# Two attention blocks on a batch of images: the order of score banks, the place of the layer statistics, and the place of the next image's norm

## The chip, the cores and the metric

The kernel runs on one core of one Trainium2 chip. The core has five engines with instruction streams of their own: TensorE (PE in the profile; its weight loads are PEld), VectorE (DVE), ScalarE (ACT), GpSimd (POOL) and SyncE (SP), which here only issues DMAs. They are tied together by semaphores. The metric is the device time of one execution in microseconds; a kernel's time is the median of several runs.

## What is computed

The input is a batch of 8 images, each 512 channels by 32 x 32 = 1024 positions, in 32-bit floats. Two attention blocks follow each other. Cut to what matters:

```
# layer 0: group norm over 32 groups, 8 heads of 64 channels
h   = group_norm(x, 32 groups)
qkv = w_qkv @ h + b_qkv                    # per image, 1x1 convolution
w   = softmax(q^T k / sqrt(64))            # per head, 1024 x 1024
x   = x + w_proj @ (w applied to v) + b_proj

# layer 1: group norm over 8 groups, one head of 512 channels
xn  = group_norm(x, 8 groups)
q, k, v = q_w @ xn + q_b, k_w @ xn + k_b, v_w @ xn + v_b
w   = softmax(q^T k / sqrt(512))
x   = x + p_w @ (w applied to v) + p_b
```

## The kernel before

**Matrix products by seven factors.** Nearly every product other than layer 0's attention is done by the scheme of Strassen and Winograd: a product of 2 x 2 blocks takes seven block products instead of eight, numbered 1 to 7, of sums and differences of blocks. `left_sums` and `right_sums` give those sums as lists of steps. `conv2` and `scores1` use the scheme twice, so that 7 outer products have 7 inner products each; `inner_steps` does the inner seven of one or two outer products, in the order 1, 6, 2, 5, 7, and leaves inner products 3 and 4 in the list `tail`. The next stage runs the tail behind its own first product (`finish`), so that TensorE has work while the first product's bank is copied. Inner products 1 and 2 use PSUM bank a, 6, 7 and 4 use b, 5 and 3 use c.

**PSUM.** Six of the eight banks are in three pools named a, b and c, two banks each, and two are in a pool `ps_acc` for small accumulations. `psum_pools` closes the three pools and opens them anew at the start of each stage, after it has run the tail. In the matrix products a tile is one bank, so each pool holds two tiles. In the attention a score tile takes the two banks of one pool, so that there are three score tiles in flight.

**Stages.** For image b, the main loop runs layer 0's attention (`attention0`), then the projection with the residual sum (`projection`), then, for image b-1, layer 1's first product g (`layer1_scores`), its scores (`scores1`), its values (`values1`), and then layer 0's values (`values`), keys and queries (`keys_and_queries`) for image b+1. For image 1 keys and queries are made in the turn of image 0, and then the function gets four hooks for the norm of layer 1. In all later turns it gets none.

**Layer 0's attention.** There are eight blocks, one for each pair of heads and half of the positions. A block makes eight score tiles (four matmul records each), takes the exponential of each on ScalarE, adds them up on VectorE, multiplies them with the values (32 matmul records), and sums over partitions (8 records). A counter n picks the pool of each score tile.

**Layer 1's statistics.** The group norm of layer 1 needs a mean and a variance of the projected image. `projection` gives them as a list `stats` of twelve steps for VectorE: eight half_stats (bn_stats over 512 positions, held in program order) and four end_stats (bn_aggr). By place in the list, 5, 7, 9 and 11 are end_stats. `scores1` deals the list out among its seven outer products. Its calls are `product(s, p, ...)`: s counts the calls, p is the number of the factor, and the fifth argument lists further factors that GpSimd makes. The argument `small` goes to the list `background`, of which one step is run behind each inner product. So a list that is given to one outer product is run from that product's inner product 6 on, one step at a time.

**Layer 0's norm of the image after next.** `values` puts the load and the statistics of image b+2 (tiles named ahead) into the background list. `keys_and_queries` then does the rest: `group_mean` is a small matmul on TensorE (gmean) and four VectorE steps on 128 x 4 numbers, `affine` is a second small matmul (gvar), one VectorE step and four GpSimd steps (the power -1/2 of the variance, the scale, the mean times scale, the shift). The scale and shift are used when that image is loaded for good and its norm is applied by ScalarE, in the turn after. A hook is a list of calls that `inner_steps` runs behind the inner product 7 of one of the four pairs of outer products of `conv2`; in the listing they are the argument `after7`.

**Order.** Instructions marked by `keep_in_program_order` keep the order in which the program writes them on their engine; all matmuls are among them. The others are placed by the builder's own scheduler.

Of the kernel before, what the change touches and what calls it, by code (L numbers as in the profile page):

```python
# [9 lines left out]
F32 = mybir.dt.float32  # L10
# [5 lines left out]
P = 128  # L16
# [13 lines left out]
def two_attention_blocks_kernel(  # L30
# [10 lines left out]
    KC = C // P  # L41
    HT = T // 2
# [29 lines left out]
    def pcols(name):  # L72
        i = 4 * PARAMS.index(name)
        return par[:, i : i + 4]
# [101 lines left out]
    def main_path(ctx):  # L176
# [14 lines left out]
        def acc_tile(name):  # L191
            return ps_acc.tile([P, HT], F32, tag="acc", name=name)


        ps_pools = []
# [408 lines left out]
        def attention0(b, q, k, v, a, extra):  # L604
            n = 0

            for hp in range(KC):
                for tb in (0, 1) if hp < KC - 1 else (1, 0):
                    uid = f"0_{b}_{hp}_{tb}"
                    total = pair_tile(f"sum_{uid}")  # L610
                    es = []
                    for s in range(NS):
                        sc = ps_pools[n % 3].tile([P, 2, HT], F32, tag="sc", name=f"sc_{uid}_{s}")
                        n += 1
                        for j in range(2):
                            matmul(
                                sc[:, j, :], k[hp][ts(j, 64), ts(s, P)], q[hp][ts(j, 64), ts(tb, HT)],
                                start=True, stop=True,
                            )
                        e = pair_tile(f"e_{uid}_{s}")  # L620
                        nc.scalar.activation(e, sc, AF.Exp, scale=(C // 8) ** -0.5)  # L621
                        if s == 1:
                            nc.vector.tensor_add(total, es[0], e)  # L623
                        elif s > 1:
                            nc.vector.tensor_add(total, total, e)  # L625
                        es.append(e)
                    for f in extra.pop(0) if extra else ():
                        f()
                    av = acc_tile(f"av_{uid}")
                    for s in range(NS):  # L630
                        for j in range(2):
                            matmul(
                                av[ts(j, 64), :], v[s // 2][:, s % 2, hp * P + j * 64 : hp * P + (j + 1) * 64],
                                es[s][:, j, :], start=(s == 0), stop=(s == NS - 1),
                            )
                    for f in extra.pop(0) if extra else ():
                        f()
                    dst = a[hp][:, ts(tb, HT)]
                    nc.scalar.copy(dst, av)  # L639

                    last = (hp, tb) == (KC - 1, 0)
                    r = reciprocals(total, uid, False, nc.scalar if last else nc.sync)
                    if not last:
                        nc.gpsimd.tensor_tensor(dst, dst, r, ALU.mult)  # L644
                    else:
                        scaled = lambda dst=dst, r=r: tc.keep_in_program_order(nc.vector.tensor_mul(dst, dst, r))

            assert not extra
            return scaled


        def scores1(f, gf, gsteps, first, uid, stats):

            scale = C**-0.5
            e = {(c, cc, r): pair_tile(f"e_{uid}_{c}{cc}{r}") for r in range(2) for c in range(2) for cc in range(2)}
            total = pair_tile(f"sum_{uid}")  # L660
            parts = [pair_tile(f"sum{r}_{uid}") for r in range(2)]
            g2 = {1: first}

            def factors(p):
                g2[p] = query_factors(gf[p], f"{p}_{uid}")

            def blocks(at, r, cc):
                return [e[at[1], cc, at[0]][:, :, ts(r, 2 * P)]]

            def add(dst, ps, x):  # L670
                nc.vector.tensor_add(dst[0], ps, x[0])  # L671

            def more(dst, x, y, r, cc):

                tc.keep_in_program_order(
                    nc.gpsimd.tensor_tensor(blocks(dst, r, cc)[0], blocks(x, r, cc)[0], blocks(y, r, cc)[0], ALU.add)
                )

            def exps(r, c):
                for cc in (1, 0):  # L680
                    nc.scalar.activation(e[c, cc, r], e[c, cc, r], AF.Exp, scale=scale)  # L681

            def add_up(r, c):

                on = lambda dst, x, y: lambda: tc.keep_in_program_order(nc.gpsimd.tensor_tensor(dst, x, y, ALU.add))  # L685
                if r == c:
                    return [on(parts[r], e[c, 0, r], e[c, 1, r])]
                return [
                    *(on(parts[r], parts[r], e[c, cc, r]) for cc in range(2)),
                    on(total[:, r, :], parts[r][:, 0, :], parts[r][:, 1, :]),  # L690
                ]

            def product(s, p, y, x, before, small, after7=(), final=()):
                def mm(ps, j, start):
                    for i in range(2):
                        matmul(
                            ps[:, i, :], f[p][j][:, ts(i, P)], g2[p][j], start=start and i == 0, stop=True, skip_group_check=True
                        )

                def extra(r, cc, read, written):  # L700

                    if p == 6 and written:
                        more((0, 1), (1, 0), (1, 1), r, cc)
                    if p == 7 and written:
                        more((1, 1), (1, 0), (1, 1), r, cc)

                inner_steps(
                    f"{uid}_{s}", s % 2, 2, mm, add, lambda *at: blocks(y, *at), x and (lambda *at: blocks(x, *at)),
                    extra, after7, final, [lambda: background.extend(small), *(lambda q=q: factors(q) for q in before)],
                )  # L710

            product(0, 1, (1, 0), None, [2], stats[:3] + gsteps[:2])
            product(1, 2, (0, 0), (1, 0), [5], gsteps[2:4], (), [lambda: exps(0, 0)])
            product(2, 5, (1, 1), None, [6, 4], gsteps[4:] + stats[3:6])
            product(3, 6, (1, 0), (1, 0), [7, 3], stats[6:7])
            product(4, 7, (1, 0), (1, 0), [], stats[7:9])
            product(5, 3, (0, 1), (0, 1), [], stats[9:11] + add_up(0, 0), [lambda: exps(1, 1)], [lambda: exps(0, 1)])
            product(
                6, 4, (1, 0), (1, 0), [], stats[11:] + add_up(1, 1) + add_up(0, 1), (),
                [lambda: exps(1, 0), lambda: background.extend(add_up(1, 0) + steps)],  # L720
            )

            t = [[pair_tile(f"t{n}_{uid}_{cc}") for cc in range(2)] for n in (1, 2, 4)]
            engines = [nc.vector] * 4 + [nc.gpsimd] * 4
            fs, steps = right_sums(
                [(e[0, cc, 0], e[0, cc, 1]) for cc in range(2)], [(e[1, cc, 0], e[1, cc, 1]) for cc in range(2)],
                [lambda cc, n=n: t[n][cc] for n in range(3)],
                lambda *a: engines.pop(0).tensor_tensor(*a, ALU.subtract),
            )
            return total, {p: [x[:, i, :] for x in fs[p] for i in range(2)] for p in fs}  # L730
# [142 lines left out]
        v, q, k, norm0, later = prologue()  # L873
# [78 lines left out]

        def keys_and_queries(b, f, norm, hooks):

            k = conv2("k", f, None, f"k0_{b}", hooks)
            hooks = [[all_background], [], []]
            if norm:
                hooks[1].append(lambda: norm.group_mean(acc_tile(f"gmean_0_{b + 1}")[:, :KC]))
                hooks[2].append(lambda: norm.affine(acc_tile(f"gvar_0_{b + 1}")[:, :KC]))
            q = conv2("q", f, pcols("bq0"), f"q0_{b}", hooks)  # L960
            return q, k

        def layer1_scores(b, inner):
# [31 lines left out]
        for b in range(B):  # L995
# [33 lines left out]
            if b > 0:  # L1029
# [4 lines left out]
                norm1, stats = projection(b, af, xt, [scaled, steps[7]])  # L1034
                gf, gsteps = layer1_scores(b - 1, inner)
                _, _, mean, affine = norm_hooks(norm1, f"1_{b}")
# [6 lines left out]
                if b + 1 < B:  # L1043
                    hf, steps = image_factors(h, f"h0_{b + 1}")
                    background.extend(steps)
                    v, f, norm0 = values(b + 1, hf)
                    q, k = keys_and_queries(b + 1, f, norm0, ())
            elif B > 1:
                v, f, norm0 = values(1, hf, [[], [], [], [], [*steps[:7], scaled, steps[7]]])
                norm1, stats = projection(0, af, xt)  # L1050
                hooks = norm_hooks(norm1, "1_0")
# [216 lines left out]
```

## Time and profile before

| What | us |
|---|---|
| median of 3 runs | 2849.69 |
| lowest and highest run | 2848.17, 2850.7 |
| the profiled execution, device time | 2849.52 |
| its span, first to last instruction | 2847.7 |
| VectorE, sum of exponentials (L623, L625) | 600.9 busy |
| ScalarE, exponentials of layer 0 (L621) | 476.8 busy |
| TensorE, layer 0's score matmuls | 458.7 busy |
| TensorE, layer 0's value matmuls | 453.6 busy |

The granted TensorE clock is 0.999 over the span. In a group of the profile, names such as `psb_q<-inner_h,w_q` give the tile written and the tiles read: `psb_q` is bank b of the queries' convolution, `sc` a score tile, `e` its exponential, `sum` the running sum, `bnst` and `mv` the statistics. Timelines give the start in us from the span's beginning, the length, the engine, the line, the operation, the tiles, the shapes and the number of instructions merged into the line; in brackets stands how long the engine was idle before it and what ended that. In rows of windows the first pair is the stretch, then its length, and then the busy time and number of instructions of each engine, the granted clock, and the share and GB/s of the DMA engines. All matmuls have line L67, as they go through one helper. One matmul of 32-bit floats has two records.

### The profile page before, as it was taken

The numbers are of one execution on the slowest core, as the hardware profiler recorded it, in microseconds if no ns is written. First come the engines' busy times: TensorE is split into PE (matmuls) and PEld (weight loads), VectorE is DVE, ScalarE is ACT, GpSimd is POOL, SyncE is SP. The second block draws the span as 40 slices with busy tenths as digits, with TensorE's granted clock in tenths as the row PEclk, the third lists the DMA queues.
The fourth block names the chain that finished last, engine by engine and source line by source line (L and its number), as shares of the span: only waits on it lengthen the run. The fifth ranks groups of instructions, "written<-read, shape, count | busy, mean of one in ns | idle before, by whom it ended". The sixth has DMA issues, their size and how long they took to land.

```text
span 2847.7 us, 32456 instructions
## 1 busy us (share of the span) xinstructions
PE 2827.0 (99%) x11846; PEld 1690.0 (59%) x11846; DVE 2083.8 (73%) x2733; ACT 929.0 (33%) x1177; POOL 1205.4 (42%) x1193
## 2 busy tenths in 40 slices
PE   9999999999999999999999999999999999999998
PEld 5435635866367653677537674376743868338584
DVE  5587787766877678776787757877578775887765
ACT  1252452214522145220552215422154311633130
POOL 2123215732167321673227722277123761147672
PEclk9999999999999999999999999999999999999999
DMA  8632403133031230322213232122311223012301
GB/s 276 190 127 90 180 20 126 36 144 134 20 144 65 106 128 26 134 94 97 109 49 111 94 118 92 49 108 97 134 72 49 107 101 142 35 52 94 121 2 68
DMA packets 91597, 280.59 MB, mean 99 GB/s; under 512 B 10595, under 2 KB 36387, under 8 KB 82470
## 3 DMA queue, kind: packets, MB, share of 16 engines
q1 hardware_dynamic: 89638, 276.15, 26.7%
q10 hardware_dynamic: 1792, 2.29, 0.2%
q8 instruction: 96, 1.57, 0.2%
q14 instruction: 71, 0.58, 0.1%
HBM read 227.31 MB, written 51.09 MB: 98 GB/s over the span
## 4 chain that ended last, share of the span: by engine, by line
PE 97%; DVE 2%; issue 1%; ACT 0%; POOL 0%; DVEq 0%; POOLq 0%; ACTq 0%
PE sc L67 16%; PE av L67 16%; PE psb_av L67 6%; PE psb L67 5%; PE psa_av L67 4%; PE psc_av L67 4%; PE psc L67 3%; PE psa L67 3%; PE psb_z L67 3%; PE psb_p L67 3%; PE psb_v L67 3%; PE psb_k L67 3%; PE psb_g L67 3%; PE psb_q L67 2%; PE psa_p L67 2%; PE psa_z L67 2%
## 5 line engine op out<-in xcount | busy, mean ns | idle before, releaser
L625 DVE TENSOR_TENSOR sum<-sum,e 128x1024 f32<-128x1024 f32 x384 | 522.4, 1360 | 41.8 <-DVE sum L623 1.4
L621 ACT ACTIVATE e<-sc 128x1024 f32<-128x1024 f32 x512 | 476.8, 1053 | 73.2 <-PE sc L67 72.3
L67 PE MATMUL sc<-q,k 64*128 64x512 f32 x2048 | 458.7, 596 | 0.5
L67 PE MATMUL av<-e,v 128*64 128x512 f32 x2048 | 453.6, 596 | 0.0
L67 PEld LDWEIGHTS sc<-q,k 64*128 64x128 f32 x2048 | 193.3, 186 | 239.2 <-ACT e L621 104.0
L67 PEld LDWEIGHTS av<-e,v 128*64 128x64 f32 x2048 | 141.4, 137 | 304.3 <-issue 304.3
L588 POOL TENSOR_TENSOR all_recs<-all_recs,rc 128x256 f32<-128x256 f32 x72 | 65.2, 905 | 528.3 <-DVE rc L586 520.7
L644 POOL TENSOR_TENSOR a<-a,r 128x512 f32<-128x512 f32 x56 | 112.6, 2010 | 265.0 <-DMA r<-rows 220.8
L586 DVE RECIPROCAL rc<-sums 128x256 f32<-128x256 f32 x72 | 126.4, 1756 | 46.4 <-PE sums L67 26.5
L532 POOL TENSOR_TENSOR k<-k,k 128x256 f32<-128x256 f32 x28 | 20.0, 727 | 315.8 <-DVE u_k L527 315.8
L639 ACT COPY a<-av 128x512 f32<-128x512 f32 x64 | 37.4, 585 | 318.2 <-PE av L67 318.2
L623 DVE TENSOR_TENSOR sum<-e,e 128x1024 f32<-128x1024 f32 x64 | 78.5, 1226 | 58.9 <-ACT e L621 58.9
L67 PE MATMUL psb<-inner,inner_h 128*128 128x256 f32 x448 | 116.1, 382 | 1.2 <-DVE u L671 0.5
L67 PE MATMUL psa_av<-e,z 128*128 128x512 f32 x256 | 113.3, 596 | 0.0
L140 ACT ACTIVATE h<-h,b,s 128x1024 f32<-128x1024 f32 x62 | 78.4, 1268 | 93.9 <-DMA h<-in_x 77.3
L411 POOL TENSOR_TENSOR inner_h<-h,inner_h 128x256 f32<-128x256 f32 x120 | 106.8, 892 | 2.2
L67 PEld LDWEIGHTS psb<-inner,inner_h 128*128 128x128 f32 x448 | 83.9, 190 | 16.9 <-POOL inner L426 3.8
L411 POOL TENSOR_TENSOR inner_h<-h 128x256 f32<-128x256 f32 x60 | 58.8, 979 | 78.5 <-ACT h L140 78.5
L685 POOL TENSOR_TENSOR sum<-sum,e 128x1024 f32<-128x1024 f32 x32 | 76.2, 2380 | 27.5 <-ACT e L681 26.2
L67 PE MATMUL psb_g<-inner_h,w_m 128*128 128x256 f32 x336 | 86.0, 383 | 0.3
L411 POOL TENSOR_TENSOR inner_h<-t_h 128x256 f32<-128x256 f32 x90 | 77.9, 868 | 10.8 <-PE psc_av L67 9.5
L67 PEld LDWEIGHTS psa_av<-e,z 128*128 128x128 f32 x256 | 48.0, 190 | 57.2 <-issue 56.6
(344 smaller groups left out, 5535.4 us busy)
## 6 DMA issues: line engine op xcount, KB each, us to landing
x<-in_x SPq DMA_DIRECT2D x36, 512.0 KB
h<-in_x SPq DMA_DIRECT2D x32, 512.0 KB
spill<-x SPq DMA_DIRECT2D x32, 512.0 KB
h<-spill SPq DMA_DIRECT2D x32, 512.0 KB
x<-spill SPq DMA_DIRECT2D x32, 512.0 KB
out<-x SPq DMA_DIRECT2D x64, 256.0 KB
w_p<-sums_p SPq DMA_DIRECT2D x8, 1792.0 KB
r<-rows SPq DMA_DIRECT2D x112, 128.0 KB
```

What stands on the lines that cost most here:

```text
L67: tc.keep_in_program_order(nc.tensor.matmul(*args, **kw))
L140: tc.keep_in_program_order(nc.scalar.activation(dst, src, AF.Identity, bias=b, scale=s))
L411: pin(nc.gpsimd.tensor_tensor(dst, x, y, ALU.subtract))
L532: nc.gpsimd.tensor_tensor(d, x, y, ALU.add)
L586: nc.vector.reciprocal(rc, sums)
L588: nc.gpsimd.tensor_tensor(all_recs, all_recs, rc, ALU.add)
L621: nc.scalar.activation(e, sc, AF.Exp, scale=(C // 8) ** -0.5)
L623: nc.vector.tensor_add(total, es[0], e)
L625: nc.vector.tensor_add(total, total, e)
L639: nc.scalar.copy(dst, av)
L644: nc.gpsimd.tensor_tensor(dst, dst, r, ALU.mult)
L685: on = lambda dst, x, y: lambda: tc.keep_in_program_order(nc.gpsimd.tensor_tensor(dst, x, y, ALU.add))
```

## The change

Three edits, all in how the same work is ordered.

1. In `attention0`, the score tile's pool is chosen by (0, 2, 1)[n % 3] instead of n % 3.
2. In `scores1`, the twelve steps of `stats` are dealt out otherwise. The call with factor 6 gets none where it had one. The call with factor 5 gets two instead of three, that with factor 7 two, that with factor 3 three instead of two, that with factor 4 two instead of one.
3. In `keys_and_queries`, where no hooks are given, the next image's `group_mean` moves from the hook behind the second pair of the queries to that behind the first pair of the keys, together with the call that empties the background list; `affine` moves from the third pair of the queries to the fourth pair of the keys. Where hooks are given (image 1), all stays.

```
-                        sc = ps_pools[n % 3].tile([P, 2, HT], F32, tag="sc", name=f"sc_{uid}_{s}")
+
+                        sc = ps_pools[(0, 2, 1)[n % 3]].tile([P, 2, HT], F32, tag="sc", name=f"sc_{uid}_{s}")
...
-            product(2, 5, (1, 1), None, [6, 4], gsteps[4:] + stats[3:6])
-            product(3, 6, (1, 0), (1, 0), [7, 3], stats[6:7])
-            product(4, 7, (1, 0), (1, 0), [], stats[7:9])
-            product(5, 3, (0, 1), (0, 1), [], stats[9:11] + add_up(0, 0), [lambda: exps(1, 1)], [lambda: exps(0, 1)])
+            product(2, 5, (1, 1), None, [6, 4], gsteps[4:] + stats[3:5])
+            product(3, 6, (1, 0), (1, 0), [7, 3], [])
+            product(4, 7, (1, 0), (1, 0), [], stats[5:7])
+            product(5, 3, (0, 1), (0, 1), [], stats[7:10] + add_up(0, 0), [lambda: exps(1, 1)], [lambda: exps(0, 1)])
             product(
-                6, 4, (1, 0), (1, 0), [], stats[11:] + add_up(1, 1) + add_up(0, 1), (),
+                6, 4, (1, 0), (1, 0), [], stats[10:] + add_up(1, 1) + add_up(0, 1), (),
...
-            k = conv2("k", f, None, f"k0_{b}", hooks)
-            hooks = [[all_background], [], []]
+            mean, affine = [], []
             if norm:
-                hooks[1].append(lambda: norm.group_mean(acc_tile(f"gmean_0_{b + 1}")[:, :KC]))
-                hooks[2].append(lambda: norm.affine(acc_tile(f"gvar_0_{b + 1}")[:, :KC]))
-            q = conv2("q", f, pcols("bq0"), f"q0_{b}", hooks)
+                mean.append(lambda: norm.group_mean(acc_tile(f"gmean_0_{b + 1}")[:, :KC]))
+                affine.append(lambda: norm.affine(acc_tile(f"gvar_0_{b + 1}")[:, :KC]))
+            if hooks:
+                k = conv2("k", f, None, f"k0_{b}", hooks)
+                q = conv2("q", f, pcols("bq0"), f"q0_{b}", [[all_background], mean, affine])
+            else:
+
+                k = conv2("k", f, None, f"k0_{b}", [[all_background, *mean], [], [], affine])
+                q = conv2("q", f, pcols("bq0"), f"q0_{b}")
             return q, k
```

## The prediction

> **What bounds the kernel now.** I read the page first, for the engine that carries the span, and then the chain of waits.
>
> ```profile
> span 2847.7 us, 32456 instructions
> PE 2827.0 (99%) x11846; PEld 1690.0 (59%) x11846; DVE 2083.8 (73%) x2733; ACT 929.0 (33%) x1177; POOL 1205.4 (42%) x1193
> PE 97%; DVE 2%; issue 1%; ACT 0%; POOL 0%; DVEq 0%; POOLq 0%; ACTq 0%
> ```
>
> TensorE is the bound from end to end: 2827.0 of 2847.7 us busy and 97% of the chain. No edit of the change takes a matmul away. So it can win only where a matmul starts late. The ends of matmuls are modelled, so late starts show in the distance between starts, not as idle time. I therefore asked for the timeline of TensorE at each place that the change touches, first the start of an attention (image 3):
>
> ```profile
> 1028.38 7.48 PE L67 MATMUL sc<-q,k 64*128 64x512 f32 x32
> 1035.79 7.09 PE L67 MATMUL av<-e,v 128*64 128x512 f32 x32
> 1042.80 0.64 PE L67 MATMUL sums<-sum,ones 128*32 128x256 f32 x8
> 1043.37 7.14 PE L67 MATMUL sc<-q,k 64*128 64x512 f32 x32
> ```
>
> A block is 32 score matmuls, 32 value matmuls and 8 for the sums. The first block's scores take 7.48 us, the next one's 7.14 us. From first score to first score, the first block takes 1043.37 - 1028.38 = 14.99 us, and the second (1058.03 in the same view) 14.66 us. Narrow timelines there show who is late:
>
> ```profile
> 1028.38 1.13 PE L67 MATMUL sc<-q,k 64*128 64x512 f32 x4
> 1028.56 0.87 DVE L525 SCALAR_TENSOR_TENSOR q<-psb_q,par,q 128x256 f32<-128x256 f32 x2
> 1029.58 0.70 PE L67 MATMUL sc<-q,k 64*128 64x512 f32 x2
> ```
>
> The first score tile, four matmuls, starts at 1028.38. The second starts at 1029.58, 1.20 us later, where one tile in the steady run takes 0.86 us (7.14 us over eight tiles, less the last matmul's modelled tail). VectorE empties bank b of the queries until 1028.56 + 0.87 = 1029.43, and the second score tile lies in b. Its start follows that end by 0.15 us.
>
> [...]so a score tile has to wait for the reader of its own bank and for no other. The trace agrees: the wait is for b, while c was empty at 1028.45. [...]the trace shows none waiting (idle before gmean and gvar 0). [...]the norm's d x d product has a median of 1.08 us, and 0.16 us where GpSimd was idle.
>
> **Part 1, the order of banks.** The rotation a, b, c becomes a, c, b; no instruction is added or removed. The queries' convolution ends with product 3 in c and then product 4 in b, so b is the last to come free. The new second tile lies in c, which VectorE leaves at 1027.57 + 0.88 = 1028.45; its turn is 1029.24 or a little later, so it does not wait. The new third tile lies in b, free for TensorE at 1029.58, and its turn is 1030.1 or later: half a microsecond of room. The gain is one late start for each attention that follows a queries' convolution through b, the seven images 1 to 7. First block against second, from the starts, they are 14.99 or 15.00 against 14.65 or 14.66 us: 0.34 us each, 7 x 0.34 = 2.4 us. The attention of image 0 follows other matmuls, and its first block already takes 14.66 us: no gain there.
>
> What is late next? ScalarE's exponentials follow each other at 0.90 us and the score tiles at 0.86, so a tile of the first block could find its bank not read yet. The steady blocks run with the same three banks and the same 0.90 us at 14.66 us a block, so the first block can become a steady one and no better. VectorE's sum of the block must end before the sums matmuls. It begins when the second exponential ends, 0.1 us earlier too, and its seven passes fit in the steady block. At the attention's end 32 value matmuls (7.1 us) lie between the last score tiles and the next user of the banks. Nothing there.
>
> **Part 2, statistics out of the product with factor 6.** One bn_stats (0.68 us on VectorE) leaves product 6, and each later one moves a product on; the last lands in the product with factor 4. The count stays twelve. Windows over layer 1's scores (window, width, TensorE busy) give the price: an image with statistics, then the last image, which has none:
>
> ```profile
> 2237.20:2277.80 40.60, 40.45 (x186) 1.00 0.12 46
> 2723.02:2763.63 40.61, 40.15 (x185) 1.00 0.00 1
> ```
>
> With or without statistics 40.6 us: VectorE has the room. No matmul of product 6 starts late. Of eight images, two take 40.73 us, from a late start in the tail of product 7, 0.13 us each; the statistic there is replaced by another one in the same slot, so I let it stay. The new last statistic stands ahead of at most two VectorE sums in the product with factor 4, whose next TensorE reader is a longer product away (eight matmuls of 0.216 us). The layer's mean comes after it with room: in image 2 the last aggregate is at 878.33 us, one product (6.0 us) later is 884.4, and the mean's matmul is at 892.73. So 0, between -0.6 (the two images' 0.13 each, and 0.34 that one image takes longer still) and +0.7 us (0.1 for each of seven images).
>
> **Part 3, the norm in the keys' convolution.** It concerns the images whose norm comes in this function without other hooks: 2 to 6, five of them. Moved are two pairs of tiny matmuls on TensorE, five small VectorE operations (0.15 to 0.20 us each), four small GpSimd ones (about 1.7 us together) and no DMA; the call that empties the background list moves too. Windows over the queries' convolution of image 6, with the norm, and of image 7, without it, then over the keys' of image 6:
>
> ```profile
> 2048.99:2073.07 24.08, 24.03 (x112) 20.09 (x110) 15.16 (x40) 7.23 (x12) 7.18 (x13) 1.00 0.64 240
> 2396.92:2420.61 23.69, 23.64 (x107) 19.63 (x106) 14.66 (x35) 7.24 (x12) 5.71 (x9) 1.00 0.64 244
> ...
> 2022.26:2048.99 26.73, 26.73 (x123) 22.96 (x122) 15.54 (x34) 4.41 (x8) 5.58 (x8) 1.00 0.33 121
> ```
>
> The norm costs the queries 24.08 - 23.69 = 0.39 us. The starts say what that is: twice 0.14 us for a pair of tiny matmuls and 0.08 us of slower start behind it, less 0.05 us where a later wait is shorter. In the keys the same two pairs cost the same. Net 0, if VectorE has room and the statistics are ready.
>
> Both are in the trace of image 3:
>
> ```profile
> 978.24 0.20 DVE L103 BATCH_NORM_AGGREGATE mv<-bnst 128x2 f32<-128x12 f32 x1
> ...
> 989.11 0.69 DVE L527 TENSOR_TENSOR k<-psb_k,c_k 128x512 f32<-128x512 f32 x1 [2.83 <-PE psb_k L67]
> 990.84 0.69 DVE L527 TENSOR_TENSOR k<-psc_k,u_k 128x512 f32<-128x512 f32 x1 [1.03 <-PE psc_k L67]
> ...
> 998.48 1.42 POOL L532 TENSOR_TENSOR k<-k,k 128x256 f32<-128x256 f32 x2 [46.33 <-DVE u_k L527]
> ```
>
> The mean's matmul would stand at 988.84, behind product 7 of the first pair; its statistics are done at 978.44, ten microseconds before. VectorE is idle 1.03 us between its two sums there, and GpSimd for 46 us, so the mean's four VectorE steps (0.74 us by their starts at 1017.20 in the queries) run unhindered and end before or just as the next sum is due. A bank emptied 0.2 us late is wanted two products later. The second half stands at the keys' last pair, where VectorE again waits 0.97 us for TensorE and GpSimd has nothing left, so the scale and shift are made sooner than now. Their reader, the next image's apply, is a whole attention away. The background list has run empty during the values' convolution (19 entries, four a step), so emptying it early adds nothing. I take 0, between -1.1 us (the stall of about 0.22 us behind the queries' third pair, five times, if the norm caused it; against that, image 7 has it too) and +1.0 us (a sum 0.2 us late, five times).
>
> **The sum.** -2.4 + 0 + 0 = -2.4 us against the profiled execution's 2849.52 us (span 2847.7 and 1.8 around it): 2847.1. That execution lies 0.17 us below the median of the runs, 2849.69, so against the median it is 2847.3, which I take: 0.08% faster. Differences within 0.2% (5.7 us) I count as the same, about what a measurement of this kernel can tell from no change.
>
> **The rivals.**
> - All parts pay. The bank's 2.4, part 2's 0.6 and part 3's 1.1 us: 2845.6. For it: VectorE is the late one in the queries' last pairs, and the norm works there. Against: image 7's starts show the same late ones without the norm. Chance 0.17.
> - The bank's gain is handed back: the score tiles then wait for exponentials, or the sums for VectorE, 2849.7. For it: 0.90 against 0.86 us. Against: the steady blocks. Chance 0.12.
> - Slower: the mean's matmul finds its statistics not ready in the keys' convolution[...]. Place: the end of the first pair of the keys. It decides from the point where the last aggregate comes after the tenth microsecond past 978.44. The load that feeds it already made VectorE wait 5.2 us in this image; a landing 12 us later would cost 2 us in each of five images: -2.4 + 10 = +7.6, 2857.3. Against: the aggregate ends within a microsecond of the keys' start in all five images. Chance 0.04.
> - Instructions that aren't held in program order find other places, since the kernel's builder orders them by its own estimate, and VectorE meets GpSimd at other times. One 7.8 us VectorE product at 943.76 us, beside a run of GpSimd subtractions, cost TensorE about 1 us in one image alone. I price it at one such event per layer-1 image, 7 us, either way: 2840.3 or 2854.3. Chance 0.12, more of it below, as the late starts that could go are many and small (0.66 us an image in the scores).
>
> **How the numbers follow.** The forecast itself has 0.55. Its own range is the three bounds added: 2847.3 - 1.7 and + 1.7, so 2845.6 to 2849.0. The range for the time takes in "all parts pay" and "handed back", with a little of the spread of the runs (2848.17 to 2850.7): 2844.6 to 2849.9. Faster by over 0.2% (below 2844.0) needs the last rival's good side, and some of the first with a low run: 0.11. Slower by over 0.2% (above 2855.4): 0.04 for the late statistics and 0.01 for the last rival's other side: 0.05. Within: 0.84.
>
> **What would show it.** Part 1 right: the first block's 32 scores read 7.14 us in all eight images, and VectorE's last sum from b ends before the third tile's turn. Handed back: a first block of 14.99 us with ScalarE or VectorE in front of the late matmul. Part 2: layer 1's scores stay at 40.6 us. Part 3: the queries at 23.69 and the keys at 27.1 us; wrong if a gmean matmul in the keys shows idle time before it. The forecast falls if the kernels differ by more than 5 us, or elsewhere than in these three places.

## The result and the profile after

The changed kernel takes 2843.98 us (median of 20 runs, 2842.68 to 2845.52), the kernel before in the same session 2849.10 us (20 runs, 2848.02 to 2851.02). The ratio is 0.9982 with a 95% interval of 0.9976 to 0.9988: 5.1 us, or 0.18%, less. The forecast had the sign, and a difference within 0.2%. But its 2847.3 us promised 2.4 us, and the result lies 0.6 us below the low end of its range, 2844.6 us. About half of the gain was not in its sum. Another 0.6 us of the distance is the base: the forecast started from a median of 2849.69 us over three runs, and twenty runs give 2849.10 us.

The page of the changed kernel, the same three lines as shown of before (span; busy time by engine; shares of the chain of waits):

```profile
span 2841.1 us, 32477 instructions
PE 2824.5 (99%) x11846; PEld 1689.7 (59%) x11846; DVE 2082.5 (73%) x2733; ACT 928.1 (33%) x1177; POOL 1201.3 (42%) x1193
PE 97%; DVE 2%; issue 1%; POOL 0%; ACT 0%; DVEq 0%; POOLq 0%; ACTq 0%
```

TensorE is still the bound, with the same 11846 matmul records, and its busy time fell by only 2.5 us while the span fell by 6.6. So part of the gain is time in which TensorE did nothing. The profiled execution took 2842.86 us, 1.1 below the median, so the 6.6 us contain some luck. One more number of the page is worth a stop: 32477 instructions against 32456, in a change that adds none in the program's text. By the records all the difference is in semaphore instructions (EVENT_SEMAPHORE): 7 more on TensorE, 17 more on ScalarE, 6 more on GpSimd, 2 fewer on VectorE and 7 fewer on SyncE.

**The place of part 1.** TensorE's timeline at the attention of image 3, in the columns start, length, engine, line, operation:

```profile
1026.17 7.14 PE L67 MATMUL sc<-q,k 64*128 64x512 f32 x32
1033.23 7.09 PE L67 MATMUL av<-e,v 128*64 128x512 f32 x32
1040.25 0.64 PE L67 MATMUL sums<-sum,ones 128*32 128x256 f32 x8
1040.82 7.14 PE L67 MATMUL sc<-q,k 64*128 64x512 f32 x32
```

The first block's scores read 7.14 us instead of 7.48, and from first score to first score the block takes 1040.82 - 1026.17 = 14.65 us, like every other. A narrow timeline around its first three score tiles (twelve records) shows why. Before:

```profile
1028.38 3.19 PE L67 MATMUL sc<-q,k 64*128 64x512 f32 x12
```

and after:

```profile
1026.17 2.85 PE L67 MATMUL sc<-q,k 64*128 64x512 f32 x12
1026.34 0.88 DVE L525 SCALAR_TENSOR_TENSOR q<-psb_q,par,q 128x256 f32<-128x256 f32 x2
```

VectorE leaves bank b at 1026.34 + 0.88 = 1027.22. The tile in b is now the third, whose turn is at least two tiles of 0.86 us after 1026.17, so at 1027.89 or later. It does not wait. Nor does the second tile, in c: in the records its first matmul starts at 1027.13, 0.09 us before VectorE leaves b. The 3.19 - 2.85 = 0.34 us are the late start. The attentions of images 1 to 7 each became 0.338 to 0.344 us shorter, 2.39 us in all; that of image 0 kept its length.

**The place of part 3.** Windows over the keys and then the queries of image 6 (stretch, its length, busy time and count on PE, PEld, DVE, ACT and POOL):

```profile
2018.69:2045.79 27.10, 27.10 (x128) 23.35 (x126) 16.25 (x38) 4.41 (x8) 5.64 (x8) 1.00 0.33 119
2045.79:2069.50 23.71, 23.66 (x110) 19.74 (x108) 14.48 (x36) 7.24 (x12) 7.26 (x12) 1.00 0.64 243
```

They read 27.10 and 23.71 us where before had 26.73 and 24.08: the norm's 0.37 us has moved from one to the other. Both were forecast, 27.1 and 23.69. And the mean's matmul finds its statistics ready, in the timeline of image 3 (two lines of TensorE):

```profile
986.63 0.28 PE L67 MATMUL gmean<-mv,gm 128*128 128x4 f32 x2
986.77 0.68 PE L67 MATMUL psa_k<-h,w_k 128*128 128x256 f32 x2
```

and the mean's steps on VectorE with the next sum behind them:

```profile
987.51 0.15 DVE L115 COPY gmean<-gmean 128x4 f32<-128x4 f32 x1
987.70 0.16 DVE L117 TENSOR_TENSOR d<-mv,gmean 128x4 f32<-128x4 f32 x1
987.89 0.16 DVE L119 TENSOR_TENSOR d<-d 128x4 f32<-128x4 f32 x1
988.09 0.16 DVE L121 TENSOR_TENSOR dv<-d,mv 128x4 f32<-128x4 f32 x1
988.85 0.69 DVE L527 TENSOR_TENSOR k<-psc_k,u_k 128x512 f32<-128x512 f32 x1 [0.60 <-PE psc_k L67]
```

No idle time stands before gmean, and the four small steps (987.51 to 988.25) fit into a hole before VectorE's next sum: VectorE still waits 0.60 us for TensorE there.

**Where the rest lies.** The starts of the stages, one after another, before against after, give the whole shift of the profile:

| Place | shift, us |
|---|---|
| first weights, before any image's work | -0.91 |
| first blocks, seven attentions | -2.39 |
| norm: keys +0.37, queries -0.37, five images | 0.00 |
| the end of image 2's layer 1 and its values | -0.62 |
| layer 1's scores, two images, 0.13 each | -0.26 |
| small ones (image 5, image 7) | -0.27 |
| from the last matmul to the end | -2.22 |
| sum | -6.67 |

The first row is spread and no gain: a second profile of the kernel before is 0.37 us shorter there, and the statistics alone, which will turn out to gain nothing, 0.91 us. Two rows are large and were not in the sum: the end of image 2 and the end of the program. The experiments are about these.

### The profile page after: what moved, and what is told of

It is laid out like the page before. It is cut to its first block, busy times and chain, and to the rows that moved or that the text cites. A ratio compares the mean times of both kernels' runs of the same rounds, so it can differ in the third digit from the quotient of the medians.

```text
span 2841.1 us, 32477 instructions
## 1 busy us (share of the span) xinstructions
PE 2824.5 (99%) x11846; PEld 1689.7 (59%) x11846; DVE 2082.5 (73%) x2733; ACT 928.1 (33%) x1177; POOL 1201.3 (42%) x1193
## 3 DMA queue, kind: packets, MB, share of 16 engines
q1 hardware_dynamic: 89638, 276.15, 27.1%
q8 instruction: 96, 1.57, 0.2%
## 4 chain that ended last, share of the span: by engine, by line
PE 97%; DVE 2%; issue 1%; POOL 0%; ACT 0%; DVEq 0%; POOLq 0%; ACTq 0%
PE sc L67 16%; PE av L67 16%; PE psb_av L67 6%; PE psb L67 5%; PE psa_av L67 4%; PE psc_av L67 4%; PE psc L67 3%; PE psa L67 3%; PE psb_z L67 3%; PE psb_p L67 3%; PE psb_v L67 3%; PE psb_k L67 3%; PE psb_g L67 3%; PE psb_q L67 2%; PE psa_p L67 2%; PE psa_z L67 2%
## 6 DMA issues: line engine op xcount, KB each, us to landing
out<-x SPq DMA_DIRECT2D x64, 256.0 KB
```

## The experiments

### Each part alone, and the kernel before once more

The first three kernels have one of the three edits shown above each; the fourth is the unchanged kernel. First theory: the bank order alone brings the attentions' 2.4 us. The rivals credit the two other parts, or the timing of the engines against each other.

```
A  sc = ps_pools[(0, 2, 1)[n % 3]].tile(...)
B  the five product(...) calls with stats[...] dealt out anew
C  keys_and_queries with mean and affine in the keys' hooks
```

> The kernel before with the new order of banks alone. Theory 1 (each part as forecast, the missing 2.5 us lies outside the three parts or in one chance collision of VectorE and GpSimd): 2.4 us faster, ratio 0.9992; first blocks of the attentions of images 1 to 7 at 14.66 us. Theory 2 (the order of banks brings all of the 5.1 us, since the shifted phase also removes the 7.8 us VectorE product of image 2): 3.4 to 5 us faster, and that long product is gone in this profile. Theory 3 (the gain comes from the norm or the statistics): under 2.4 us.

> The kernel before with the new dealing of the layer-1 statistics alone. Theory 1: 0.3 us faster (two images of eight lose a late start of 0.13 us), ratio 0.9999, not to be told from no change; scores at 40.60 us in all images. Theory 3: 1 us or more faster. The 7.8 us VectorE product of image 2 stays under theory 1, unless it is a matter of chance from run to run.

> The kernel before with the norm moved to the keys alone. Theory 1: no change, ratio 1.0000; keys 26.73 + 0.45 us, queries 24.08 - 0.45 us. Theory 3: 1.5 to 2.5 us faster, either there or because the 7.8 us VectorE product of image 2 is gone.

> The kernel before, unchanged, against itself. Ratio 1.0000 within 0.0003 gives what a comparison of this kernel can tell. Its profile shows what in the first one is chance: under theory 1 the start (first matmuls of the weights, 0.98 us between the two profiles) and the end (6.96 us after VectorE's last operation against 4.74 us) differ from run to run; if they stay at the values of the first profile of the kernel before, they belong to the program.

The ratios are to the kernel before, run beside them.

| Kernel | median, us | ratio to before (2848.75 us) | span, us |
|---|---|---|---|
| bank order alone | 2844.57 | 0.9986 (0.9979 to 0.9992) | 2843.3 |
| statistics alone | 2848.16 | 0.9997 (0.9989 to 1.0006) | 2846.6 |
| norm alone | 2848.27 | 0.9998 (0.9990 to 1.0007) | 2847.0 |
| unchanged | 2849.0 | 1.0000 (0.9991 to 1.0008) | 2847.7 |

Parts 2 and 3 alone cannot be told from nothing. The bank order alone gives 4.2 us, nearly the whole gain. That is the size that theory 2 expected but not its cause, since the long VectorE product of image 2 is still there (7.81 us at 942.88). Its stage starts hold only the forecast 2.4 us in the seven attentions and 0.2 us elsewhere, up to the last matmul. The remaining 1.8 us of its profile come after that matmul. So the question was no longer which part, but what happens at the end. The timeline's last matmul and last VectorE instruction, before:

```profile
2838.46 0.19 PE L67 MATMUL ps_good<-ones,both 128*1 128x1 f32 x2
2840.02 0.75 DVE L748 SCALAR_TENSOR_TENSOR x<-o,obias,x 128x512 f32<-128x512 f32 x1
```

and with the bank order alone (the timeline's head gives the span, which is 2847.7 us before):

```profile
core 0 of [0], span 2843.3 us
...
2835.84 0.19 PE L67 MATMUL ps_good<-ones,both 128*1 128x1 f32 x2
2837.40 0.75 DVE L748 SCALAR_TENSOR_TENSOR x<-o,obias,x 128x512 f32<-128x512 f32 x1
```

VectorE's last sum ends 2.31 us after the last matmul's start in both (2840.02 + 0.75 - 2838.46; 2837.40 + 0.75 - 2835.84). But from there to the end of the span it is 2847.7 - 2840.77 = 6.9 us before, and 2843.3 - 2838.15 = 5.2 us with the new order. No calculation lies there; what runs is the end of TensorE's own program. Its instructions that do no arithmetic are in the trace, though not in the timelines. In us from the start of TensorE's last matmul record, which lies 0.03 us behind the start in the timeline, as records of the trace:

```
before        TENSOR_LOAD 0.86  COMPARE_BRANCH 1.46 (3.61 long)  EVENT_SEMAPHORE 5.12  DRAIN 8.49  EVENT_SEMAPHORE 8.67 ... end 9.25
bank order    TENSOR_LOAD 0.86  COMPARE_BRANCH 1.45 (3.75 long)  EVENT_SEMAPHORE 5.26  DRAIN 5.41  EVENT_SEMAPHORE 6.84 ... end 7.42
```

Before, 3.4 us pass between a semaphore instruction of 0.05 us and the next instruction; with the new order 0.15 us. The second profile of the unchanged kernel has the long end too (9.74 us), so it is not chance from run to run. And the counts of TensorE's records differ: 24085 before, 24092 with the bank order. The difference is seven EVENT_SEMAPHORE instructions (388 and 395), one in each attention of images 1 to 7. Where the second score tile alone waited for its bank in an instruction of its own (at 1029.47 in image 3), now the second and the third do (1027.72 and 1028.70 with the bank order alone). The statistics alone and the norm alone leave 24085.

This suggested that the end depends on where TensorE's last instructions lie in the packets of the queue for instructions. The page has "q8 instruction: 96, 1.57", packets and MB; by the records each packet has 16384 bytes. The first 94 of them go out one behind another while TensorE runs: in the kernel before, the first when 196 of its instructions have started and the 94th when 24005 have, so one packet in every 256.0 instructions on average (139 to 366 from one to the next); in the changed kernel 194 and 23979, one in every 255.8. From this comes an estimate: one packet stands for a block of 256 of TensorE's instructions. 24085 instructions at 256 a block are a little over 94 blocks, beside 96 packets.

The records of this queue hold the packets' times too. In us from the last matmul record again, the last two packets and what TensorE did next:

```
before        packet 2.47 to 3.66, branch ends 5.07;  packet 5.82 to 7.29, DRAIN 8.49
bank order    packet 2.46 to 3.74, branch ends 5.20;  DRAIN 5.41, packet 5.94 to 6.91
```

The first of these packets goes out during the branch in all thirteen profiles of this document, and the branch ends 1.4 to 1.5 us after it has landed. The second packet goes out in all of them too. Before, the DRAIN follows its landing by 1.2 us; with the bank order the DRAIN has run before this packet goes out. So the gap of the kernel before ends as the branch does, shortly after a packet has landed.

### Shifting the instructions without touching the work

If only the place in the block counts, a few instructions put ahead of the kernel before must shorten its end, with the banks in the old order. Two small matmuls whose result nothing reads were added before the first stage, 8 records in all. The three pairs of parts were run beside it.

```
+        for i in range(2):
+            matmul(acc_tile(f"pad{i}")[:, 0:1], ones, ones[:, 0:1], start=True, stop=True)
```

> The kernel before with two tiny matmuls added ahead of the first weights, while TensorE waits for its first load; nothing reads their result. They only make TensorE's program a few instructions longer, as the new order of banks does (seven semaphore instructions more on TensorE). Theory 1 (the 2.2 us at the end is a place in the program[...]): the end after the last matmul falls from 9.3 to 9.8 us to 7.0 to 7.5 us, and the kernel gets 2 us faster, ratio 0.9993, without any of the three edits. Theory 2 (the shorter end comes from the order of banks itself, or is chance): end and time as before, ratio 1.0000.

> Bank order and statistics, norm as before. Theory 1: 2.4 us (seven first blocks) + 2.2 us (end) + up to 0.3 us: ratio 0.9983 to 0.9985. The 7.8 us VectorE product in image 2, 1 us of TensorE time, is there in all kernels but the changed one: if it is a matter of phase between VectorE and GpSimd, it can be gone or not; if one pair of edits removes it, this is the pair or one of the next two.

> Bank order and norm, statistics as before. Theory 1: 2.4 + 2.2 us and nothing from the norm: ratio 0.9984 to 0.9985; end after the last matmul 7.0 to 7.5 us. With the 7.8 us VectorE product gone 1 us more.

> Statistics and norm, bank order as before. Theory 1: no gain from the first blocks (15.0 us still) and none at the end (9.3 to 9.8 us after the last matmul): ratio 0.9997 to 1.0000. If the 7.8 us VectorE product is gone here, it goes with these two edits together, and the ratio is 0.9995.

| Kernel | median, us | ratio to before (2848.56 us) | span, us | last matmul to end, us |
|---|---|---|---|---|
| before with two small matmuls | 2846.48 | 0.9991 (0.9983 to 1.0000) | 2845.2 | 7.45 |
| banks and statistics | 2843.68 | 0.9982 (0.9975 to 0.9990) | 2841.6 | 7.54 |
| banks and norm | 2843.80 | 0.9984 (0.9977 to 0.9992) | 2843.0 | 7.47 |
| statistics and norm | 2847.85 | 0.9997 (0.9988 to 1.0005) | 2846.5 | 9.08 |

Two useless matmuls made the kernel before 2.1 us faster. The time alone would hardly tell that from nothing, as its interval touches 1; the records do. The end of its timeline (span, last matmul, last VectorE instruction):

```profile
core 0 of [0], span 2845.2 us
...
2837.72 0.19 PE L67 MATMUL ps_good<-ones,both 128*1 128x1 f32 x2
2839.28 0.75 DVE L748 SCALAR_TENSOR_TENSOR x<-o,obias,x 128x512 f32<-128x512 f32 x1
```

After VectorE's last instruction, 2845.2 - 2840.03 = 5.2 us are left, as with the bank order. So far every kernel with the new bank order has the short end, and every one without it and without added matmuls the long one: 9.25 and 9.74 us (before, twice), 9.72 (statistics), 9.79 (norm), 9.08 (both), against 7.42, 7.54, 7.47 and, in the changed kernel, 7.03 us.

### Both at once, and a shift of almost a whole block

If the short end can only be won once, the bank order on top of the two small matmuls gives its 2.4 us and no more. And if the block is what counts, 62 one-column matmuls (248 records) must bring the long end back in the changed kernel, since 7 + 248 = 255 is one short of the estimated block of 256: the border that lay ahead of the first DRAIN would then lie one instruction behind it. In the kernel before, 248 alone puts the border eight instructions behind the DRAIN, past the last ones, and the end must be short.

```
+        for i in range(62):
+            if i % 31 == 0:
+                pad = acc_tile(f"pad{i}")
+            matmul(pad[0:1, 0:1], ones[:, 0:1], ones[:, 0:1], start=True, stop=True)
```

> The kernel before with the two tiny matmuls at the start and the new order of banks: the gain of the banks with the end already short. Theory 1: against the padded kernel before (2846.5 us) 2.4 us faster for the seven first blocks, so 2844.1 us, ratio to the kernel before 0.9984 to 0.9985, and no faster than the order of banks alone (2844.6 us); end after the last matmul 7.0 to 7.5 us. Theory 2 (the order of banks is worth over 4 us by itself): 2842.3 us.

> The changed kernel with 62 matmuls of one column and one row at the start, whose result nothing reads. Each is four instructions in the records, so TensorE's program grows by 248; with the seven of the changed kernel that is 255[...]. Theory 1: the last instructions lie across a block again, and the end after the last matmul is 9 to 10 us where it was 7.03. Theory 2: it stays at 7.0 to 7.5. The start may be some us later.

> The kernel before with the same 62 matmuls: 248 instructions more, eight short of a whole block. Theory 1: its last instructions, five or six, end before the block does, so the end after the last matmul is 7.0 to 7.5 us where it was 9.25 to 9.74. Theory 2: it stays at 9.2 to 9.8.

The bank order on top of the two matmuls took 2844.26 us (ratio to before 0.9985, 0.9979 to 0.9992), 2.2 us below the 2846.48 us of the two matmuls alone. That is the attentions' 2.4 us within what the medians can tell, and the end is not paid for a second time (6.99 us from the last matmul to the end). With 62 matmuls ahead of the changed kernel (one execution, 2845.95 us) the end of its timeline is long again:

```profile
core 0 of [0], span 2844.2 us
...
2835.63 0.19 PE L67 MATMUL ps_good<-ones,both 128*1 128x1 f32 x2
2837.19 0.75 DVE L749 SCALAR_TENSOR_TENSOR x<-o,obias,x 128x512 f32<-128x512 f32 x1
```

From 2837.94 to 2844.2 it is 6.3 us, where the changed kernel has 2841.1 - 2836.3 = 4.7:

```profile
2834.02 0.19 PE L67 MATMUL ps_good<-ones,both 128*1 128x1 f32 x2
2835.58 0.75 DVE L749 SCALAR_TENSOR_TENSOR x<-o,obias,x 128x512 f32<-128x512 f32 x1
```

In the records the gap came back one instruction later than in the kernel before, as one instruction less than a block asks:

```
before, as it is         EVENT_SEMAPHORE 5.12  DRAIN 8.49  EVENT_SEMAPHORE 8.67 ... end 9.25
before + 62 matmuls      EVENT_SEMAPHORE 5.13  DRAIN 5.28  EVENT_SEMAPHORE 6.89 ... end 7.47
after, as it is          EVENT_SEMAPHORE 4.98  DRAIN 5.20  EVENT_SEMAPHORE 6.45 ... end 7.03
after + 62 matmuls       EVENT_SEMAPHORE 4.96  DRAIN 5.11  EVENT_SEMAPHORE 8.13 ... end 8.51
```

So the two borders lie 255 + 1 = 256 instructions apart, as the packets do on average.

The long end of 8.51 us is smaller than the 9 to 10 us expected: its gap is 3.0 us where that of the kernel before is 3.4 us, and behind the gap 0.38 us are left where there were 0.76 us. In the kernels with a short end another 1.2 to 1.8 us pass behind the first DRAIN. In the kernel before only 0.18 us pass there (8.49 to 8.67), behind the gap, and so a gap of 3.0 to 3.6 us costs only about 2 us.

The kernel before with 62 matmuls has the short end, 7.47 us. Its one execution still took 2849.0 us (span 2847.0), as its last matmul came 1.1 us later than in the kernel before; 0.8 us of that come from a second product of the kind that the next part shows.

The queue's count agrees. The page of the kernel before has 96 instruction packets:

```profile
q8 instruction: 96, 1.57, 0.2%
```

The pages of the two kernels with 248 more instructions on TensorE, and of no other, have one more in this queue, while the other instruction queue, q14, keeps its 71 packets:

```profile
q8 instruction: 97, 1.59, 0.2%
```

So the place in the block is shown as the cause, by shifting it in both directions. That the gap is a wait for the packet is read from the times in the records: in all six profiles with a long end the late instruction starts 1.2 to 1.4 us after the last packet has landed, and in the seven with a short end the first DRAIN starts before that packet goes out.

### The long VectorE product

The row of -0.62 us at the end of image 2 is one VectorE instruction. VectorE's timeline there, before:

```profile
943.04 0.69 DVE L745 TENSOR_TENSOR o<-psc_av,w_av 128x512 f32<-128x512 f32 x1
943.76 7.81 DVE L746 TENSOR_TENSOR o<-o,r 128x512 f32<-128x512 f32 x1
951.61 1.09 DVE L748 SCALAR_TENSOR_TENSOR x<-o,obias,x 128x512 f32<-128x512 f32 x1
```

GpSimd's, before:

```profile
943.46 0.73 POOL L411 TENSOR_TENSOR inner_h<-h 128x256 f32<-128x256 f32 x1
944.14 0.72 POOL L411 TENSOR_TENSOR inner_h<-h,h 128x256 f32<-128x256 f32 x1
944.83 0.72 POOL L411 TENSOR_TENSOR inner_h<-h,inner_h 128x256 f32<-128x256 f32 x1
```

VectorE's, after:

```profile
941.66 0.69 DVE L746 TENSOR_TENSOR o<-psc_av,w_av 128x512 f32<-128x512 f32 x1
942.39 0.69 DVE L747 TENSOR_TENSOR o<-o,r 128x512 f32<-128x512 f32 x1
943.12 1.10 DVE L749 SCALAR_TENSOR_TENSOR x<-o,obias,x 128x512 f32<-128x512 f32 x1
```

GpSimd's, after:

```profile
941.80 0.73 POOL L411 TENSOR_TENSOR inner_h<-h,h 128x256 f32<-128x256 f32 x1
942.49 1.18 POOL L411 TENSOR_TENSOR inner_h<-h,inner_h 128x256 f32<-128x256 f32 x1
943.63 1.17 POOL L411 TENSOR_TENSOR inner_h<-h 128x256 f32<-128x256 f32 x1
```

The same instruction takes 0.69 us when it starts 0.59 us into a GpSimd subtraction (942.39 - 941.80), and 7.81 us when it starts 0.30 us into one (943.76 - 943.46): then subtraction after subtraction runs at its own 0.72 us, and VectorE stands through some eleven of them.

The thirteen traces together show how far the moment of the start decides. They hold 185 products of this line (`o<-o,r`) that start while such a subtraction runs. Twelve of them start 0.27 to 0.31 us into it, and eleven of the twelve took 7.8 us. The other 173 start earlier or later, and none took more than 1.31 us. The twelfth, in the kernel with two matmuls and the bank order, started 0.30 us in and took 0.98 us, so the moment alone does not decide, and what else does is open.

No single edit removes the long product. It is in image 2 in both executions of the kernel before (7.80 us at 943.44 in the second), with each part alone (7.79 to 7.82 us), with banks and norm (7.80 us) and in the kernel before with two matmuls (7.83 us). It is absent with banks and statistics. The bank order has it when alone, and has none with the two small matmuls ahead. With statistics and norm it has left image 2 for image 5 (two stretches of VectorE's timeline there):

```profile
943.25 0.71 DVE L746 TENSOR_TENSOR o<-o,r 128x512 f32<-128x512 f32 x1
...
1987.56 7.84 DVE L746 TENSOR_TENSOR o<-o,r 128x512 f32<-128x512 f32 x1
```

Without the event TensorE's next start moves forward by 1.03 us, of which 0.4 lies the other way in the stages around it. The changed kernel has no product of this length, but with 62 matmuls at its start, which touch neither VectorE nor GpSimd, it has one in image 5 (7.83 us at 1986.48). The kernel before with the same 62 matmuls has two (943.99 and 1989.50). So it is luck that the changed kernel has none. No run held the event apart from everything else: 0.6 us is less than the medians can tell.

## Why the prediction was wrong in size

**Part 1, the late start: right, to the hundredth.** Seven times 0.34 us were forecast and 2.39 us measured, in the places named, with the steady block as the limit.

**Part 1, "no instruction is added or removed": this step failed.** It is true of what the program writes, and false of what TensorE runs. In the records one score tile of an attention waited for its bank in an instruction of its own, and with the new order two do: seven instructions more (395 EVENT_SEMAPHORE on TensorE where there were 388). The count alone costs nothing that shows in the stages. But the forecast counted only what moves ahead of the last matmul, and put the stretch from there to the end of the span at no change without a reason. The seven instructions moved the end of TensorE's program past the border of a block, 256 instructions by the distance of the packets and by the shift of 255. The missing term is that stretch: -2.2 us in the profile, -2.1 us by the medians with two useless matmuls in its place. Added to the forecast's 2847.3 us it gives 2845.2, inside the range. The text's own sign of being wrong, a difference of more than 5 us or one elsewhere than in its three places, came true on both counts. That the edit which wins 2.4 us in the attentions also adds the instructions that win 2 us at the end is luck: two useless matmuls did the same.

**Part 2: right.** Forecast 0 with -0.6 to +0.7 us. The statistics alone measure 0.9997 (0.9989 to 1.0006). The two late starts of 0.13 us in layer 1's scores did go, where the text had let them stay. They also went with the norm alone, and so are not the work of this part in particular; the one image that takes 0.34 us longer stays in the changed kernel and is gone with the statistics or with the norm alone.

**Part 3: right.** Net 0 was forecast, and less than 0.01 us measured in four of the five images, with keys and queries at the lengths given. In image 3 the keys take 0.19 us more. That is not the norm's, for the norm alone has none of it, and the bank order with the statistics, without the norm, has 0.34 us; the table counts it with the end of image 2. The slower rival, statistics that come late, has nothing for it: gmean waits in none of the images, and what a late one would hold up was not shown. The forecast's median of 1.08 us for the d x d product is no time that the product takes: of the sixteen in the trace before, eight took 0.16 us and eight 2.0 to 2.3 us. In the keys it takes 0.16 us.

**The rival of VectorE meeting GpSimd at other times: its event came true, its price didn't.** It named the product at 943.76 us, and that product did fall out. It was priced at one event in each image, 7 us; it was one event in one image, 0.6 us. Its low side was right in direction, and this is the second term that was missing.

**"All parts pay"**, 2845.6 us, came nearest in time for a reason that does not hold: parts 2 and 3 pay nothing that can be told from zero. Together the sum reads -2.4 (attentions) - 2.1 (end) - 0.6 (the long product) - 0.3 (scores) = -5.4 us, against -5.1 us measured; the difference is less than the half-width of the interval of the unchanged kernel against itself, 0.0008 or 2.3 us.

No version was found that beats the changed kernel: banks and statistics without the norm, at 2843.68 us, is the same within its interval.

## What to carry to other kernels

When a change of a few microseconds is judged, look at the program's end before crediting the edit: compare the distance from the last matmul to the end of the span, and the number of instructions on the bounding engine, waits included. A change of 2 us can be put to the test with a handful of useless instructions ahead of the unchanged kernel; if these win as much, the edit did not. And when a bank is handed from one stage to the next, let the stage's first users take the banks in the order in which they come free: this gained the 0.34 us of each late start, and nothing was late in its place.

## What the runs showed of the hardware

- The end of the program has a price that depends on the number of TensorE's instructions: 9.1 to 9.8 us from the last matmul to the end in five profiles with 24085 records, 7.0 to 7.5 us in seven with 7 to 15 or 248 more, and 8.5 us with 255 more. In the six long ends TensorE's next instruction starts 1.2 to 1.4 us after a 16384-byte instruction packet has landed, 3.0 to 3.6 us after the instruction before it. In all thirteen the branch ahead took 3.4 to 3.9 us, and ended 1.4 to 1.5 us after the landing of another such packet.
- A VectorE product of two operands in SBUF, 0.69 us by itself, stood 7.8 us behind back-to-back GpSimd subtractions in eleven of the twelve cases in which it started 0.27 to 0.31 us into one, and took 0.69 to 1.31 us in the 173 cases in which it started at another moment. While it stood, GpSimd ran at its undisturbed 0.72 us; where it did not stand, the next subtraction took 1.18 us in the case shown.
